# A two-layer graph kernel: layer 0's normalised rows transposed by DMA in place of TensorE, their head projection placed 20 blocks later, and the first attention selections on other buffers

## The chip, the cores and the metric

The kernel runs on one core of a Trainium2 chip. The metric is the device time of one execution in microseconds (us). Before the change it is 2277.46 us, the median of 3 runs (2276.98 to 2278.27).

The core's engines work side by side, each through its own queue in order: TensorE (PE in the profile; PEld is its weight load), VectorE (DVE), ScalarE (ACT), GpSimd (POOL) and SyncE (SP). SyncE and GpSimd issue the DMAs here, which run on 16 DMA engines.

## The reference

There are N = 3327 nodes with 1024 features each, and a sparse weighted adjacency `adj` (3327 x 3327). Two layers, each with a residual:

```python
# layer 0
h = maximum(layernorm(x), 0)
s = quant4(relu(quant4(h) @ quant(W0)))             # small integers
x1 = x + (adj / asf) @ s * (asf * delta)
# layer 1: attention with 8 heads of 64, over the edges of adj
h   = maximum(layernorm(x1), 0)
Wh  = einsum('nf,hfd->hnd', h, W)                   # 1024 -> 8 x 64
e   = leaky_relu(a1.Wh[i] + a2.Wh[j], 0.2), only where adj[i, j] > 0
out = elu(softmax(e) @ Wh)                          # then a dense part of four layers
x2  = x1 + mlp(out)
```

The change is about the step between the two layers: `layernorm(x1)`, its relu, and `Wh`.

## The kernel before, in words

Nodes are cut into T = 26 tiles of 128 rows. The work comes in four stages.

**Stage 1** (0 to 135 us): the quantised product of layer 0, `s_int[t]` for all 26 tiles, kept in SBUF. Its rows are transposed by DMA (line 300) as 128x1024 two-byte words.

**Stage 2** (135 to 974 us): for each tile t, `x1[t]` is the adjacency product: 26 blocks j, and in each block 4 matmuls of 128x512 (line 532): the adjacency block is split into a high and a low part (`hi`, `lo`) so that two fast passes give the accuracy, times two column halves. The blocks come in PARTS of 7, 6, 7 and 6. For each part the adjacency is loaded (`at`, three buffers, SyncE, line 183), `hi` is cast on ScalarE (line 187), `lo` and the 0/1 mask `mk` are made on VectorE (191, 192); `hi` and `lo` have two buffers each, so that `hi` of a part waits until TensorE is done with the part two before it. After a tile's blocks: `y` on ScalarE (547), then on VectorE a scale (548), the residual (549), the statistics and `half_normalised` (149 to 156), which gives (x1 - mean) / (2 sd).

`heads(t, y)` (line 463) then makes `Wh`: eight 128x128 TensorE transposes into PSUM (469), two evictions with relu and a factor of 2 into `ht` (470), eight 128x512 fp32 matmuls (473, two passes each) into `whm`, an eviction `wht` (475), the scores `src` and `dst` on VectorE (480, 481), a transpose of `src` (487), the exponentials (485, 497) and the features `ft`, `fw`, `dw` (498 to 511), written to DRAM by GpSimd (`src_d`, `feat_d`, `dsum_d`). The loop at 522 runs one tile behind: heads(t-1) is issued after tile t-1's normalisation and runs on TensorE among the first blocks of the next tile. A scheduler sets the order within each engine's queue when the program is built; `keep_in_program_order` fixes single instructions.

**Stage 3** (974 to 1976 us): attention. For each of 32 attends (a head and a group of 6 or 7 tiles), 26 steps j: VectorE makes `sel` (line 826, the mask where the score passes the leaky-relu's kink), TensorE multiplies it by the features `f_even` or `f_odd` into 7 accumulators (835). Between them come the edge sums (`all_edges`, 613): masks cast to `mf` on ScalarE (635) and multiplied by `dw` (636); `edge_steps(n)` (647) says how many of them are due by step n. The stage's loads are in SyncE's queue: masks of the first group, the source scores `srow` (601), features and sums of the tiles that are done, further masks, and the last tiles' features when they are written. They go to memory that `s_int` gives up, and to pools that follow stage 2's.

**Stage 4** (1976 us to the end): the dense part and the output.

Of the kernel before, what the change touches and what calls it, by code (L numbers as in the profile page):

```python
# [1 line left out]

# [6 lines left out]
F32 = mybir.dt.float32  # L9
BF16 = mybir.dt.bfloat16  # L10
F32R = mybir.dt.float32r
U8 = mybir.dt.uint8
I8 = mybir.dt.int8
AF = mybir.ActivationFunctionType
ALU = mybir.AluOpType
AX = mybir.AxisListType
PSUM = bass.MemoryType.PSUM
DRAM = bass.MemoryType.DRAM

P = 128  # L20
# [3 lines left out]
TH = T // 2  # L24
# [35 lines left out]
def two_layer_kernel(  # L60
# [83 lines left out]
    def plus_eps(var, n, tag, engine=nc.vector):  # L144
        v = small.tile([P, n], F32, tag=tag + "v", name=tag + "v")
        engine.tensor_scalar(v, var, EPS, None, ALU.add)
        return v

    def half_normalised(dst, src):

        stats = small.tile([P, FC, 6], F32, tag="stats", name="stats")
        statistics(stats, src)
        mv = small.tile([P, 2], F32, tag="mv", name="mv")
        nc.vector.bn_aggr(mv, stats.rearrange("p c s -> p (c s)"))
        r = half_inverse(plus_eps(mv[:, 1:2], 1, "ln"), 1, "ln")
        nc.vector.tensor_scalar(dst, src, mv[:, 0:1], r, ALU.subtract, ALU.mult)

    def scale_and_bias(rs, mean, n, factor, tag, engine=nc.vector):

        nb = small.tile([P, n], F32, tag=f"{tag}n", name=f"{tag}n")  # L160
        if engine is nc.vector:
            nc.vector.tensor_scalar(rs, rs, factor, None, ALU.mult)
            nc.vector.scalar_tensor_tensor(nb, mean, -1.0, rs, ALU.mult, ALU.mult)
        else:
            engine.tensor_scalar(rs, rs, factor, -1.0, ALU.mult, ALU.mult)
            engine.tensor_tensor(nb, mean, rs, ALU.mult)
            engine.tensor_scalar(rs, rs, -1.0, None, ALU.mult)
        return rs, nb

# [4 lines left out]
    with tc.tile_pool(name="at", bufs=2, reuse_waits="tile") as atp:  # L176
# [276 lines left out]
        with tc.tile_pool(name="wh", bufs=1, reuse_waits="tile") as whp, tc.tile_pool(  # L453
            name="s2", bufs=2, reuse_waits="tile"
        ) as s2, tc.tile_pool(name="mm", bufs=2, space=PSUM, reuse_waits="tile") as mm_ps, tc.tile_pool(
            name="s2_tp", bufs=2, space=PSUM, reuse_waits="tile"
        ) as tp_ps, tc.tile_pool(name="s2_wh", bufs=2, space=PSUM, reuse_waits="tile") as wh_ps:

            whead = whp.tile([P, KF, EMB], F32, name="whead")
            a1_t = whp.tile([P, EMB], F32, name="a1_t")  # L460
            a2_t = whp.tile([P, EMB], F32, name="a2_t")

            def heads(t, h):
                ht = s2.tile([P, KF, P], F32, name="ht", bufs=1)
                for g in range(KF // 4):
                    tp = tp_ps.tile([P, 4, P], F32, tag="tp2", name="tp2")
                    for q in range(4):
                        k = 4 * g + q
                        nc.tensor.transpose(tp[:, q, :], h[:, k * P : (k + 1) * P], ident)
                    nc.scalar.activation(ht[:, 4 * g : 4 * g + 4, :], tp, AF.Relu, scale=2.0)  # L470
                whm = wh_ps.tile([P, EMB], F32, name="whm")
                for k in range(KF):
                    nc.tensor.matmul(whm, ht[:, k, :], whead[:, k, :], start=(k == 0), stop=(k == KF - 1))  # L473
                wht = s2.tile([P, EMB], F32, name="wht", bufs=1)
                nc.scalar.copy(wht, whm)
                src = small.tile([P, NH], F32, name="src")
                dst = small.tile([P, NH], F32, name="dst")
                for a_t, e in ((a1_t, src), (a2_t, dst)):
# [4 lines left out]
                    )  # L483
                nc.vector.tensor_scalar(ndst[:, t], dst, -1.0, None, ALU.mult)
                nc.scalar.activation(ratio[:, t], src, AF.Exp, scale=1.0 - SLOPE)
                sp = tp_ps.tile([P, 4, P], F32, tag="tp2", name="sp")
                nc.tensor.transpose(sp[:NH, 0, :], src, ident)
                srct = s2.tile([NH, P], F32, name="srct")
                nc.scalar.copy(srct, sp[:NH, 0, :])  # L489
                for sub, d in zip(SUBS, src_d):  # L490
                    if t in sub:
                        nc.gpsimd.dma_start(d[:, (t - sub[0]) * P : (t - sub[0] + 1) * P], srct)
# [29 lines left out]
            for t in range(T):  # L522
                xt = s2.tile([P, F], F32, name="xt2")
                load_rows(xt, x, t)
                mm = mm_ps.tile([P, F], F32, tag="mm", name="mm2")
                for js in PARTS:
                    hi, lo = part
                    part = next(columns, None)
                    for q, j in enumerate(js):
                        for which in (hi, lo):  # L530
                            for c in range(FC):
                                nc.tensor.matmul(  # L532
                                    mm[:, c * 512 : (c + 1) * 512],
                                    which[:, q, :],
                                    s_int[j][:, c * 512 : (c + 1) * 512],
                                    start=(j == 0 and which is hi),
                                    stop=(j == T - 1 and which is lo),
                                )
                if t == 0:
                    for dst, ap in (  # L540
                        (whead, w_heads.rearrange("(k p) e -> p k e", p=P)),
                        (a1_t, a1.partition_broadcast(P)),
                        (a2_t, a2.partition_broadcast(P)),
                    ):
                        tc.keep_in_program_order(nc.sync.dma_start(dst, ap))
                y = s2.tile([P, F], F32, name="y")
                nc.scalar.activation(y, mm, AF.Copy, scale=r_asf)
                nc.vector.tensor_scalar(y, y, asf_t, sup_delta, ALU.mult, ALU.mult)
                nc.vector.tensor_tensor(xt, xt, y, ALU.add)
                nc.gpsimd.dma_start(x1_d[t * P : (t + 1) * P, :], xt)  # L550
                half_normalised(y, xt)
                if before is not None:
                    heads(*before)
                before = (t, y)
            heads(*before)
    supp.close()

# [9 lines left out]
    attends = [(c, g, e, si) for c, g in units for e in range(2) for si in range(2)]  # L567
    STEPS = 4 * T
    EDGE = 13 * T
    START = T - 2  # L570
    FRONT = 6
    LATE = 62
# [5 lines left out]
    dw = large(early, "dw", [P, T, HW], F32R)  # L578
    f_even = large(early, "f_even", [P, T, HW], F32R)
    masks[0] = large(early, "mask0", [P, 7, T, P], U8)  # L580
    with tc.tile_pool(name="sel", bufs=4, reuse_waits="tile") as selp, tc.tile_pool(
        name="srow", bufs=2, reuse_waits="tile"
    ) as srowp, tc.tile_pool(name="mf", bufs=2, reuse_waits="tile") as mfp, tc.tile_pool(
        name="md", bufs=2, reuse_waits="tile"
    ) as mdp, tc.tile_pool(name="f1", bufs=1, reuse_waits="tile") as f1p, tc.tile_pool(
        name="s3", bufs=1, reuse_waits="tile"
# [14 lines left out]
        def load_src(i):  # L601
            c, g, e, si = attends[i]
            nb = len(halves[c][si])
            srow = srowp.tile([P, 7, P], F32, name="srow")
            nc.sync.dma_start(
                srow[:, :nb].rearrange("p b i -> p (b i)"),
                src_d[2 * c + si][2 * g + e].partition_broadcast(P),
            )
            return srow

        def all_edges():

            for u, (c, g) in enumerate(units):
# [13 lines left out]
                for i in range(len(blocks)):  # L627
# [3 lines left out]
                    ps = m_ps.tile([P, 512], F32, tag="mps", name="mps")[:, :HW]  # L631
                    for j in range(T):
                        if j % TH == 0:
                            mf = mfp.tile([P, TH, P], F32R, tag="mf", name="mf")
                            nc.scalar.copy(mf, mask[:, j : j + TH, :])  # L635
                        nc.tensor.matmul(ps, mf[:, j % TH, :], dw[:, j, :], start=(j == 0), stop=(j == T - 1))  # L636
                        if j == T - 1:
# [9 lines left out]
        def edge_steps(n):  # L647

            if n < START:
                return min(n, START)  # L650
            if n < LATE:
                return START + (EDGE - START) * (n - START) // (LATE - START)
            u = min((n - LATE) // STEPS, len(units) - 2)
            m = n - LATE - STEPS * u
            span = STEPS + (LAST if u == len(units) - 2 else 0)

            first = min(T, max(0, (m - 6) * 2))
            rest = (EDGE - T) * max(0, m - 19) // (span - 19)
            return EDGE * (u + 1) + first + min(rest, EDGE - T)

# [59 lines left out]

        old, young = PARTS[:3], [range(20, 24), range(24, 25), range(25, 26)]
        load_mask(0, SUBS[0])
        srow = load_src(0)
        load_features(f_even, feat_d, 0, old)
        load_features(dw, dsum_d, 0, old)
        load_mask(1, SUBS[1])
        for js in young:
            load_features(f_even, feat_d, 0, [js])
            load_features(dw, dsum_d, 0, [js])
        load_features(f_odd, feat_d, 1, old + young)  # L730
        for i, (c, g, e, si) in enumerate(attends):
            if i == len(attends) - 1:

# [74 lines left out]
            sub, mask = halves[c][si], masks[si]  # L808
            nb = len(sub)
            f = f_odd if e else f_even  # L810
            srow_next = load_src(i + 1) if i + 1 < len(attends) else None
            accs = [acc_ps.tile([P, HW], F32, tag="acc", name="acc") for _ in sub]
            for j in range(T):
                n = i * T + j
# [7 lines left out]
                if n in (STEPS * NPAIR - T, STEPS * NPAIR):  # L822
                    si1 = (n - (STEPS * NPAIR - T)) // T
                    load_mask(si1, halves[1][si1])
                sel = selp.tile([P, 7, P], F32R, tag="sel", name="sel")
                nc.vector.scalar_tensor_tensor(  # L826
                    sel[:, :nb],
                    srow[:, :nb],
                    ndst[:, j, h : h + 1],
                    mask[:, :, j, :],  # L830
                    ALU.is_gt,
                    ALU.mult,
                )
                for b in range(nb):
                    nc.tensor.matmul(  # L835
                        accs[b], sel[:, b, :], f[:, j, :], start=(j == 0), stop=(j == T - 1)
# [125 lines left out]
```

## Time and profile before

| what | value |
|---|---|
| runs, median of 3 | 2277.46 us |
| the profiled execution's own time | 2277.77 us |
| its span | 2276.0 us |
| TensorE busy | 2219.2 us |
| VectorE, ScalarE, GpSimd busy | 1538.1, 978.7, 143.6 us |
| stage 2, one tile of 26 | 31.8 us |
| adjacency matmuls, line 532 | 2704 of 128x512 |
| heads' matmuls, line 473 | 416 passes of 128x512 |
| heads' TensorE transposes, line 469 | 208 of 128x128 |
| their evictions, line 470 | 52, mean 592 ns |
| DMA traffic | 311.47 MB, 137 GB/s over the span |
| granted TensorE clock, mean | 0.997 |

A group line of the profile gives the line of the code, the engine and operation, output <- inputs, shapes and count, then total busy time and the mean in ns of one, then the idle time of the engine ahead of them and what ended it. A line of the order of time gives start and length in us from the span's start, with runs of one kind merged. A TensorE matmul's length is longer than its spacing, since matmuls are pipelined: spacing is read from the starts. A line by windows gives, for each stretch, the busy us and the instructions of PE, PEld, DVE, ACT and POOL, then the granted TensorE clock (1.00 is full), the DMA share and GB/s.

### The profile page before, as it was taken

To read this page: it belongs to the slowest core of one execution; us is meant where nothing else is said; L and a number is where in the kernel's file an instruction comes from. 1 tells how busy PE (TensorE), PEld (TensorE's weight loads), DVE (VectorE), ACT (ScalarE), POOL (GpSimd) and SP (SyncE) were. 2 spreads that over 40 slices of the span, in tenths; PEclk is the share of its full clock that TensorE was granted. 3 is DMA by queue.
4 is the path that set the end of the run, shared out by engine and by line. 5 is a ranking of instruction groups with operands and counts; after the bars stand their busy time and mean duration, and the time that the engine had idled before them with its cause. 6 is when DMAs were issued, how large, how long until landed. Compare 5 with 4: busy or idle time off the path is not lost. (4 is left out here: it accounts for less than half of the span.)

```text
span 2276.0 us, 31632 instructions
## 1 busy us (share of the span) xinstructions
PE 2219.2 (98%) x12688; PEld 1772.3 (78%) x12696; DVE 1538.1 (68%) x1963; ACT 978.7 (43%) x1640; POOL 143.6 (6%) x241
## 2 busy tenths in 40 slices
PE   4999999999999999899999999999999999999998
PEld 1467777777777777589999999999999999744444
DVE  7745545555555455487999999999999999732211
ACT  5633333433343333346555555555555555311110
POOL 1300101011010111000000000000000000000000
PEclk9999999999999999999999999999999999999999
DMA  6854444454444544754233141654242422333311
GB/s 208 207 188 134 159 144 159 134 164 151 150 152 139 167 146 152 261 176 137 85 114 112 60 134 55 226 174 149 85 146 84 137 85 75 127 143 126 120 56 56
DMA packets 176579, 311.47 MB, mean 137 GB/s; under 512 B 36452, under 2 KB 117300, under 8 KB 176432
## 3 DMA queue, kind: packets, MB, share of 16 engines
q1 hardware_dynamic: 156648, 236.28, 32.0%
q0 software_dynamic: 19776, 73.17, 10.0%
q8 instruction: 99, 1.62, 0.3%
q14 instruction: 48, 0.39, 0.1%
q10 hardware_dynamic: 8, 0.00, 0.0%
HBM read 216.07 MB, written 86.79 MB: 133 GB/s over the span
## 5 line engine op out<-in xcount | busy, mean ns | idle before, releaser
L826 DVE SCALAR_TENSOR_TENSOR sel<-srow,ndst,mask 128x896 fp32r<-128x896 f32 (+1 forms) x832 | 864.1, 1080 | 51.4 <-PE acc L835 38.7
L636 PE MATMUL mps<-dw,mf 128*128 128x260 f32 x2704 | 454.9, 283 | 0.1
L532 PE MATMUL mm<-s_int,hi 128*128 128x512 f32 x1352 | 432.9, 399 | 0.0
L532 PE MATMUL mm<-s_int,lo 128*128 128x512 f32 x1352 | 421.8, 391 | 0.0
L835 PE MATMUL acc<-f_even,sel 128*128 128x260 f32 x2704 | 397.1, 284 | 0.1
L835 PE MATMUL acc<-f_odd,sel 128*128 128x260 f32 x2704 | 394.5, 286 | 0.0
L635 ACT CAST mf<-mask 128x1664 fp32r<-128x1664 uint8 x208 | 331.3, 1593 | 124.0 <-PE mps L636 101.2
L636 PEld LDWEIGHTS mps<-dw,mf 128*128 128x128 f32 x2704 | 378.2, 188 | 0.3 <-ACT part L640 0.3
L835 PEld LDWEIGHTS acc<-f_odd,sel 128*128 128x128 f32 x2704 | 352.8, 188 | 7.3 <-issue 3.4
L835 PEld LDWEIGHTS acc<-f_even,sel 128*128 128x128 f32 x2704 | 355.1, 188 | 2.9 <-ACT srct L489 0.3
L532 PEld LDWEIGHTS mm<-s_int,lo 128*128 128x128 f32 x1352 | 253.8, 188 | 57.6 <-issue 5.7
L532 PEld LDWEIGHTS mm<-s_int,hi 128*128 128x128 f32 x1352 | 252.1, 188 | 55.7 <-issue 5.7
L192 DVE TENSOR_SCALAR mk<-at 128x896 uint8<-128x896 f32 (+1 forms) x104 | 61.5, 593 | 257.2 <-DMA at<-in_adj_t 256.3
L187 ACT CAST hi<-at 128x896 fp32r<-128x896 f32 x104 | 92.6, 891 | 328.9 <-PE mm L532 294.8
L473 PE MATMUL whm<-whead,ht 128*128 128x512 f32 x416 | 187.1, 603 | 0.8 <-ACT ht L470 0.8
L906 PE MATMUL o<-weights,h 128*128 128x512 f32 x416 | 179.7, 592 | 0.0
L906 PEld LDWEIGHTS o<-weights,h 128*128 128x128 f32 x416 | 79.0, 190 | 99.1 <-issue 98.8
L473 PEld LDWEIGHTS whm<-whead,ht 128*128 128x128 f32 x416 | 77.5, 191 | 98.2 <-issue 88.1
L191 DVE TENSOR_TENSOR lo<-at,hi 128x896 fp32r<-128x896 f32 x104 | 106.6, 1025 | 58.9 <-ACT hi L187 49.4
L640 ACT COPY part<-mps 128x260 f32<-128x260 f32 x104 | 39.2, 377 | 221.5 <-PE mps L636 221.5
L916 DVE TENSOR_TENSOR yo<-o,nodes 128x1024 f32<-128x1024 f32 (+1 forms) x27 | 31.9, 1184 | 138.2 <-PE o L906 138.0
L423 PE MATMUL mm<-w_int,xqt 128*128 128x512 bf16 x408 | 95.4, 386 | 14.8 <-ACT sb L449 4.8
(154 smaller groups left out, 1519.7 us busy)
## 6 DMA issues: line engine op xcount, KB each, us to landing
feat_d<-fw POOLq DMA_DIRECT2D x26, 1040.0 KB, 5.4
f_even<-feat_d SPq DMA_DIRECT2D x7, 3380.0 KB, 13.3
f_odd<-feat_d SPq DMA_DIRECT2D x7, 3380.0 KB, 12.7
at<-in_adj_t SPq DMA_DIRECT2D x52, 448.0 KB, 4.4
at<-in_adj_t SPq DMA_DIRECT2D x52, 384.0 KB, 3.2
mask<-mask_d SPq DMA_DIRECT2D x39, 416.0 KB, 7.4
dw<-dsum_d SPq DMA_DIRECT2D x16, 910.0 KB, 8.8
dsum_d<-dw POOLq DMA_DIRECT2D x26, 520.0 KB, 6.5
```

The source lines that it names most:

```text
L187: ins = nc.scalar.copy(hi, at)
L191: nc.vector.tensor_tensor(lo, at, hi.bitcast(F32), ALU.subtract)
L192: ins = nc.vector.tensor_scalar(mk[:, r], at, 0.0, None, ALU.is_gt)
L423: nc.tensor.matmul(mm[:, r], xqts[t][:, k, :], w_int[:, k, r], start=(k == 0), stop=(k == KF - 1))
L473: nc.tensor.matmul(whm, ht[:, k, :], whead[:, k, :], start=(k == 0), stop=(k == KF - 1))
L532: nc.tensor.matmul(mm[:, c * 512 : (c + 1) * 512], which[:, q, :], s_int[j][:, c * 512 : (c + 1) * 512], start=(j == 0 and which is hi), s ...
L635: nc.scalar.copy(mf, mask[:, j : j + TH, :])
L636: nc.tensor.matmul(ps, mf[:, j % TH, :], dw[:, j, :], start=(j == 0), stop=(j == T - 1))
L640: nc.scalar.copy(part[:, i % 7], ps.rearrange("p (q c) -> p q c", q=2))
L826: nc.vector.scalar_tensor_tensor(sel[:, :nb], srow[:, :nb], ndst[:, j, h : h + 1], mask[:, :, j, :], ALU.is_gt, ALU.mult,)
L835: nc.tensor.matmul(accs[b], sel[:, b, :], f[:, j, :], start=(j == 0), stop=(j == T - 1))
L906: nc.tensor.matmul(ps[:, c * 512 : (c + 1) * 512], h3[:, k, q * P : (q + 1) * P], w4[:, k, c * 512 : (c + 1) * 512], start=(k == 0), stop= ...
```

## The change

It has these parts.

1. The normalised row is no longer scaled ahead of the projection: `normalised` makes max(x1 - mean, 0) in one VectorE instruction before the inverse deviation is known, and returns the factor r beside it; r is applied where `whm` is evicted.
2. For tiles 0 to 24 the row is transposed by DMA. DMA transposes two-byte words here, and the row is fp32, so ScalarE copies the row's 16-bit halves apart (`yh`, 128x2048 words), SyncE transposes them (`yht`), and ScalarE puts the halves together again (`ht`). Tile 25 keeps the TensorE transposes.
3. `heads(t-1)` is issued ahead of the last part of tile t, so after 20 of 26 blocks, and its first matmul and the eviction `wht` are held there.
4. PSUM: the transposes' pool goes; `sp` gets a bank of its own, and tile 25's transposes, `whm` and `sp` take turns in one bank. The buffer of `y` is single instead of double.
5. Stage 3: the pools of `mf`, `srow` and `sel` are laid out so that the first ones lie on the adjacency's buffers; `srow` is loaded ahead of the features; the edge sums begin at step 10, two a step; from step 4 on the first attend's selections are held behind tile 25's normalisation (`ln`).

In the queues of the built program, TensorE's order for a tile in the middle of stage 2 changes as follows (numbers are matmuls; the score transpose is `sp`).

```
before: transposes 8, adjacency 5, heads 8, adjacency 10, sp 1, adjacency 89
after:  adjacency 80, heads 8, adjacency 10, sp 1, adjacency 14
```

ScalarE's order for a tile after: `hi`, `fw`, `y`, `dw` twice, `hi`, `yh`, square root, `hi`, `ht`, `hi`, `wht`, exponentials. SyncE's: four `at`, the transpose, the x row.

```diff
-    def half_normalised(dst, src):
+    def normalised(dst, src):
         stats = small.tile([P, FC, 6], F32, tag="stats", name="stats")
         statistics(stats, src)
         mv = small.tile([P, 2], F32, tag="mv", name="mv")
         nc.vector.bn_aggr(mv, stats.rearrange("p c s -> p (c s)"))
+        ins = nc.vector.tensor_scalar(dst, src, mv[:, 0:1], 0.0, ALU.subtract, ALU.max)
         r = half_inverse(plus_eps(mv[:, 1:2], 1, "ln"), 1, "ln")
-        nc.vector.tensor_scalar(dst, src, mv[:, 0:1], r, ALU.subtract, ALU.mult)
+        nc.vector.tensor_scalar(r, r, 2.0, None, ALU.mult)
+        return ins, r
...
+    def halves_of_words(words):
+        return words.bitcast(U16).rearrange("p (n two) -> p two n", two=2)
...
+            def transposed_by_dma(y):
+                yh = s2.tile([P, 2, F], U16, name="yh", bufs=1)
+                nc.scalar.copy(yh, halves_of_words(y))
+                yht = s2.tile([P, 2 * KF, P], U16, name="yht", bufs=1)
+                nc.sync.dma_start_transpose(yht, yh.rearrange("p two f -> p (two f)"))
+                ht = s2.tile([P, KF, P], F32, name="ht", bufs=1)
+                nc.scalar.copy(
+                    halves_of_words(ht.rearrange("p k i -> p (k i)")),
+                    yht.rearrange("p (two k) i -> p two (k i)", two=2),
+                )
+                return ht
+            def transposed_by_tensor(y):
                 ht = s2.tile([P, KF, P], F32, name="ht", bufs=1)
                 for g in range(KF // 4):
-                    tp = tp_ps.tile([P, 4, P], F32, tag="tp2", name="tp2")
+                    tp = last_ps.tile([P, 4, P], F32, tag="last", name="tp2")
...
-                    nc.scalar.activation(ht[:, 4 * g : 4 * g + 4, :], tp, AF.Relu, scale=2.0)
-                whm = wh_ps.tile([P, EMB], F32, name="whm")
+                    nc.scalar.copy(ht[:, 4 * g : 4 * g + 4, :], tp)
+                return ht
+            def heads(t, ht, r):
+                if t == T - 1:
+                    whm, sp = (last_ps.tile([P, EMB], F32, tag="last", name=n) for n in ("whm", "sp"))
+                else:
+                    whm = wh_ps.tile([P, EMB], F32, name="whm")
+                    sp = sp_ps.tile([P, EMB], F32, name="sp")
                 for k in range(KF):
...
+                    if k == 0 and t < T - 1:
+                        tc.keep_in_program_order(ins)
                 wht = s2.tile([P, EMB], F32, name="wht", bufs=1)
-                nc.scalar.copy(wht, whm)
+                ins = nc.scalar.activation(wht, whm, AF.Copy, scale=r)
+                if t < T - 1:
+                    tc.keep_in_program_order(ins)
...
                 for js in PARTS:
                     hi, lo = part
                     part = next(columns, None)
+                    if js is PARTS[-1] and before is not None:
+                        heads(*before)
...
-                half_normalised(y, xt)
-                if before is not None:
-                    heads(*before)
-                before = (t, y)
+                ln, r = normalised(y, xt)
+                before = t, (transposed_by_tensor if t == T - 1 else transposed_by_dma)(y), r
             heads(*before)
...
+    FIRST = 10
...
-                return min(n, START)
+                return min(max(0, n - FIRST) * 2, START)
...
-        srow = load_src(0)
-        load_features(f_even, feat_d, 0, old)
+        srow, ins = load_src(0)
+        with tc.issue_after(ins.ins):
+            load_features(f_even, feat_d, 0, old)
...
+                with tc.issue_after(ln.ins) if i == 0 and j >= 4 else nullcontext():
+                    nc.vector.scalar_tensor_tensor(
```

## The prediction

> **What bounds the kernel now.** I read the page's first two parts, then the stage's groups by shape, then the order of time on TensorE across one tile boundary of layer 0 and across the passage to the attention stage, and last the DMA rows that stand nearest to what is new.
>
> ```profile
> PE 2219.2 (98%) x12688; PEld 1772.3 (78%) x12696; DVE 1538.1 (68%) x1963; ACT 978.7 (43%) x1640; POOL 143.6 (6%) x241
> ...
> PE   4999999999999999899999999999999999999998
> ```
>
> TensorE (PE) is busy 98% of the span, the others leave room. So time is won only where TensorE instructions go away or where it idles. It idles in slice 0 (the start, untouched) and in slice 16 (counted from 0), where the passage to attention begins at 945 us.
>
> ```profile
> 436.64 1.03 PE L469 MATMUL tp<-ident,y 128*128 128x128 f32 x8
> 437.43 0.71 PE L532 MATMUL mm<-s_int,hi 128*128 128x512 f32 x2
> 437.98 0.62 PE L532 MATMUL mm<-s_int,lo 128*128 128x512 f32 x2
> 438.44 0.39 PE L532 MATMUL mm<-s_int,hi 128*128 128x512 f32 x1
> 438.77 7.13 PE L473 MATMUL whm<-whead,ht 128*128 128x512 f32 x16
> 445.34 0.79 PE L532 MATMUL mm<-s_int,hi 128*128 128x512 f32 x1
> ...
> 468.44 1.03 PE L469 MATMUL tp<-ident,y 128*128 128x128 f32 x8
> ```
>
> One period of layer 0 (columns: start, length, line): 31.8 us from one row's transposes to the next. Starts matter, ends overlap. The eight transposes hold TensorE from 436.64 to 437.43, 0.79 us, and the pair behind them takes 0.55 where its fellows take 0.45. So a row's transposes cost 0.79 to 0.89 us, nothing beside them. (Near the end of the span 16 of the same kind take 1.75: 0.875 for eight. I use that.)
>
> ```profile
> 945.00:955.00 10.00, 8.73 (x28) 4.15 (x26) 3.69 (x6) 3.98 (x6) 0.55 (x1) 1.00 1.08 362
> 955.00:965.00 10.00, 1.49 (x8) 1.52 (x9) 7.09 (x11) 2.09 (x5) 0.54 (x1) 0.68 1.06 381
> 965.00:975.00 10.00, 9.28 (x19) 3.78 (x17) 3.48 (x7) 4.12 (x8) 1.69 (x2) 0.81 0.98 344
> ```
>
> The passage, ten us a row: busy us of PE, weight loads, VectorE (DVE), ScalarE (ACT), GpSimd; then granted clock, DMA share, GB/s. The last adjacency matmul ends at 945.57. Tile 24's heads fill until 954.6, then TensorE stands until 963.5: VectorE's first selection waits for the row of source scores (landed 957.9, the DMA queues are full), and tile 25's layer norm stands behind it.
>
> **The change, part by part.**
>
> *Transposes out of TensorE.* 25 of 26 rows: 25 x 0.875 = 21.9 us off TensorE. This is all on the path, if nothing new is late. The order of the built kernel shows it: each row now has 80 adjacency matmuls, 8 of the heads, 10 more, the score transpose, 14 more, in place of "8 transposes, 5, heads, 10, score transpose, 89".
>
> *Is the row's transposed copy there by block 20?* Let S be the tile's first matmul; a block is 4 matmuls of 0.2266 (pairs start every 0.453): 0.906. Heads are due at S + 18.1. The chain, by row durations in the order in which each engine's queue now has them: ScalarE: hi of the second part to S+0.6, fw 1.06, y 1.11, to S+2.8. VectorE: y 0.81, add 1.23, a mask 0.63, two statistics 1.29, aggregate 0.20, subtract 0.81, to S+8.05. ScalarE's hi of the third part stands ahead of the copy of halves and waits for block 7 (S+6.3, done 7.1), so the copy starts at 8.1.
>
> The two copies of 128x2048 16-bit words are not in the trace. The casts of 896 and 768 elements (945 and 837 ns) give 0.84 ns an element and 190 fixed, 1.91 us for 2048. One-byte input is no quicker (1664 in 1593, formula 1588) and gaps cost nothing (dw<-fw 520 in 631, formula 627), so below 1.9 there is no reason, and above it only if 16-bit halves went at half rate, 3.6. I take 1.91. The first copy ends at S+10.0.
>
> The nearest row for the DMA is layer 0's first product, which transposes 128x1024 two-byte words:
>
> ```profile
> L300 SPq DMA_TRANSPOSE xqt<-xq x25: 1231/1232/2122, 30.9 to 121.4; - x25
> ...
> DMA to landing us min/median/max: 3.1/3.1/6.8
> ```
>
> Issuing holds SyncE's queue 1.23 us, landing 3.1 from the start of issue. Twice the words: 2.46 to issue, and 2.46 + (3.1 - 1.23) = 4.35 to land; with the worst of the 25, 6.8 + 1.2 = 8. [...] I take 4.35[...]. Landing at S+14.4, second copy to S+16.4: 1.7 us before the heads are due. So no wait; the cover is thin, and each us beyond a landing of 6.05 costs 25 us.
>
> *Who is queued behind the new waits.* SyncE: the transpose waits for the copy (S+10.0) and holds the queue to 12.5; behind it are the next tile's x row and the adjacency parts, which in the trace arrive well over a tile part before use (three buffers): free. ScalarE: the second copy waits for the DMA; behind it is hi of the next part, which cannot start before S+17.9 anyway: free. Its added work is 2 x 1.91 less two evictions of 0.6, 2.6 us a tile on 11.9 of 31: free. VectorE: one more tensor_scalar (0.15 to 0.2): free. The lo of the third part comes at S+9.4 instead of earlier, due at 11.8. The score transpose keeps its 10 matmuls of cover, as now. GpSimd's queue keeps its order. DMA: the stage 100 to 122 us, mostly transposes, shows share 0.55 at 110 GB/s where 155 GB/s here is 0.47; I add about 0.1: free on average.
>
> *The passage.* Tile 24's heads now lie inside tile 25's blocks, so they no longer cover the passage, but the first selections can: they use the adjacency's buffers, the source scores are loaded ahead of the features, and four selections are allowed before tile 25's subtract. I compare lost time = elapsed less TensorE work, from the last adjacency matmul to the end of the first attend (182 matmuls).
> Before: 945.57 to 1006.2, 60.6 us. Work: two heads with transposes 15.7, 229 matmuls of 260 columns at 0.12, 27.4; lost 17.6.
> After, T = the last adjacency matmul: VectorE bounds it. It starts at T+1.6 (fw of tile 24, y on ScalarE), and has y 0.85, add 1.26, statistics 1.6, subtract 0.85, 26 selections at about 1.12 (1.15 alone, 1.05 chained) 29.1, scores 2.9, ft 1.3, fw 1.3, small ones 1.4: 40.6. It runs dry for 3.5 us while TensorE is in tile 25's heads (T+12.9 to 19.8; four selection buffers). The sum is T+45.7. Work: 0.9 + 6.9 + 0.1 + 212 x 0.12 = 33.3. Lost 12.4.
> The clock: [...] this trace, after 9 us of standstill, shows grants of 0.68 and 0.81 and those heads at 8.80 us instead of 6.87: 1.9 more. I take the trace: lost 14.4. Gain 17.6 - 14.4 = 3.2[...], and I lean up by 1 because some matmuls do run in those 13 us: 4.2.
> Masks and scores for the first selection: three or four of seven mask loads, and the scores, now stand behind tile 24's transpose on SyncE, to S+12.5; 2.1 MB at the 257 to 362 GB/s of these windows is 6 to 8 us, S+21; needed at T+3.4 = S+34. Free.
> *Edge sums.* They start 10 steps later, at two a step; the same number is done by step 24. Already in the work counts.
>
> **Sum.** 21.9 + 4.2 = 26.1. The profiled execution took 2277.77 (span 2276.0, 1.8 around it): 2251.7. The median of the runs, 2277.46, lies 0.3 lower: 2251.4.
>
> **Rivals.**
> 1. *The likeliest, as above*, 2245 to 2257: 0.63. For it: 13 or more of 25 transposes at the minimum of 3.1.
> 2. *Short waits in each tile* (landing 6.3 to 7, or ScalarE's order a little later than worked out): 0.3 to 0.9 us a row. At 0.6, 15 us: 2266. For it: feature writes, a 384 KB adjacency load and the transpose are under way together. 0.16.
> 3. *Slower*: the transpose lands late each tile, and TensorE waits ahead of the heads at block 20. The point from which it decides: 26.1 / 25 = 1.04 us of wait, a landing of 7.1 us after issue. At the row's worst, scaled to 8, the wait is 1.95 and 25 x 1.95 = 49: 2300. For it: the 6.8 in the row; copies at half rate would do the same. Against: median equals minimum while 512 KB loads were under way. 0.09.
> 4. *Passage no better*: first selection waits for its masks on VectorE, ahead of tile 25's statistics, as now. 4 to 8 us lost: 2257. 0.12. Against: 13 us of slack.
> That the order isn't as said is excluded by the built order.
>
> **Numbers.** Within 0.2% (4.6 us, about what a measurement can tell from no change) is 2273 to 2282. Faster: case 1, 4, and nearly all of 2: 0.88. Same: 0.04. Slower: 0.08. The range: below 2244 only if the passage loses half of what I reckon; above, case 2 up to 2268; left out are case 3 and tails.
>
> **What would show it.** No TensorE transposes in layer 0 but tile 25's; a period of 30.9 us; no wait of the heads on the second copy. Copies 1.9 us each. Transposes landing 4 to 6 us after issue. Between the last adjacency matmul and the first attend's end 46 to 48 us, TensorE starting selections within 5. Wrong if the heads wait, if the period stays near 31.8, or if VectorE's first selection waits for a DMA.

## The result, and the profile after

The changed kernel takes 2258.87 us, the median of 4 runs (2256.93 to 2262.46), beside 2277.86 (2276.98 to 2278.30) before: a ratio of 0.9918, 95% interval 0.9905 to 0.9932. The gain is 19.0 us; forecast were 26.1 (2251.4), with a range up to 2268. The profiled execution took 2258.69, its span is 2256.9.

The page's busy times:

```profile
PE 2199.3 (97%) x12496; PEld 1753.9 (78%) x12496; DVE 1532.4 (68%) x1989; ACT 1062.0 (47%) x1642; POOL 145.0 (6%) x241
```

TensorE has 19.9 us less work. ScalarE has 83 us more, and it hurts nowhere by its sum. One period of layer 0, in order of time on TensorE (start, length, line), without a wait:

```profile
488.92 7.03 PE L502 MATMUL whm<-whead,ht 128*128 128x512 f32 x16
495.38 1.03 PE L568 MATMUL mm<-s_int,hi 128*128 128x512 f32 x2
...
519.64 7.03 PE L502 MATMUL whm<-whead,ht 128*128 128x512 f32 x16
```

From heads to heads 30.72 us, where before it was 31.81. Not every row goes like that; the heads of another row, which wait 1.10 us, and the sum over TensorE's waits (us in total, times, longest):

```profile
769.35 7.13 PE L502 MATMUL whm<-whead,ht 128*128 128x512 f32 x16 [1.10 <-ACT ht L479]
```

```profile
PE whm L502 <- ACT ht L479: 6.8, 10, 2.1
PE acc L876 <- issue: 5.0, 1, 5.0
```

In 10 of 25 rows the heads wait for the joined row. The 24 periods from the first heads to the 25th sum to 747.4 us, 10.1 more than 24 x 30.72. That is more than the 6.8 of the waits: behind a wait the heads start from an idle TensorE and take up to 6.57 us to the next adjacency matmul in place of 6.46, and a wait's idle time counts only from the modelled end of the matmul before it. The chain that ends there, by line 477 (issue of the transpose in ns, then landing, min/median/max) and by ScalarE's two copies (busy us and mean ns ahead of the idle time):

```profile
L477 SPq DMA_TRANSPOSE yht<-yh x25: 3246/3630/5720, 167.9 to 914.3; - x25
...
DMA to landing us min/median/max: 5.2/5.8/8.1
```

```profile
L479 ACT COPY ht<-yht 128x2048 uint16<-128x2048 uint16 x25 | 62.6, 2506 | 85.5 <-DMA yht<-yh 85.5
L475 ACT COPY yh<-y 128x2048 uint16<-128x2048 uint16 x25 | 47.5, 1900 | 20.7 <-DVE y L156 20.7
```

The first copy has its 1.91 us. The second takes 2.51 in place of 1.91, and the transpose lands after 5.8 in place of 4.35. (The trace has the landings of 17 of the 25; the joining copies, of all 25, begin 5.8 us after the issue in the median.) The row is later than reckoned by 0.6 + 1.45 = 2.05, somewhat more than the slack of 1.7: in the median the joined row is complete 18.1 us after the tile's first matmul, just when the heads are due.

The passage, ten us a row (busy PE, weight loads, VectorE, ScalarE, GpSimd, then granted clock, DMA share, GB/s):

```profile
935.00:945.00 10.00, 4.67 (x20) 3.59 (x19) 8.72 (x13) 6.19 (x8) 2.68 (x4) 0.77 1.09 359
945.00:955.00 10.00, 9.87 (x42) 7.74 (x43) 7.27 (x12) 1.38 (x3) 0.00 (x0) 0.71 1.03 411
```

The last adjacency matmul ends at 937.37, the first selection's matmuls begin at 942.53, 5.2 us later (5.0 by the trace's count of idle time), and the hole of 9 us is gone. From the last adjacency matmul to the end of the first attend (182 selection matmuls) it is 47.0 us, before 59.3 when counted alike. Tile 24's heads and transposes (7.6) and 14 matmuls of edge sums at 0.12 (1.7) have left that stretch, so the passage itself gained 12.3 - 9.3 = 3.0.

### The profile page after: what moved, and what is told of

Read it like the earlier page. It is cut to its first block, busy times and chain, and to the rows that moved or that the text cites. A ratio compares the mean times of both kernels' runs of the same rounds, so it can differ in the third digit from the quotient of the medians.

```text
span 2256.9 us, 31286 instructions
## 1 busy us (share of the span) xinstructions
PE 2199.3 (97%) x12496; PEld 1753.9 (78%) x12496; DVE 1532.4 (68%) x1989; ACT 1062.0 (47%) x1642; POOL 145.0 (6%) x241
## 5 line engine op out<-in xcount | busy, mean ns | idle before, releaser
L568 PE MATMUL mm<-s_int,hi 128*128 128x512 f32 x1352 | 427.1, 397 | 0.0
L957 DVE TENSOR_TENSOR yo<-o,nodes 128x1024 f32<-128x1024 f32 (+1 forms) x27 | 31.8, 1182 | 137.6 <-PE o L947 137.4
## 6 DMA issues: line engine op xcount, KB each, us to landing
f_even<-feat_d SPq DMA_DIRECT2D x7, 3380.0 KB, 12.3
```

Source lines behind the costliest of these rows:

```text
L568: nc.tensor.matmul(mm[:, c * 512 : (c + 1) * 512], which[:, q, :], s_int[j][:, c * 512 : (c + 1) * 512], start=(j == 0 and which is hi), s ...
```

## The experiments

Twelve kernels beside the changed one. Theory A: what the forecast lacks is the row's late arrival, by the transposing DMA (what shares the DMA engines with it, or its size) and by the joining copy. Rival: TensorE's saving was over-reckoned, or the passage gave less. (Letters in the expectations stand for the theories as they stood when each was written.)

**Heads three blocks later.** 2.7 us more cover, if nothing else moves.

```diff
-                    if js is PARTS[-1] and before is not None:
-                        heads(*before)
                     for q, j in enumerate(js):
+                        if js is PARTS[-1] and q == (3 if t < T - 1 else 0) and before is not None:
+                            heads(*before)
```

> The heads of tiles 0 to 23 stand 3 blocks later (after 23 of 26); tile 24's stay at block 20, everything else as in the changed kernel. Theory A (the row's transposed copy comes late for block 20, because the DMA transpose takes 5.8 us to land instead of 4.35 and the joining copy 2.5 instead of 1.91): 3 blocks are 2.7 us of cover, more than the longest wait of 2.1, so the waits of TensorE on the joining copy (8.8 us in all by the gaps before the heads) go, all but tile 24's 1.4: 2258.9 - 7.4 = 2251.5, every period 30.8, and the spread of the runs shrinks. Rival B (the copy is late because the stage's engines or DMA queues are loaded, and what is waiting moves along with the heads): waits of like size at the new place, 2257 to 2259.

2296.5 us (2291.94 to 2297.8), ratio 1.0076 (1.0062 to 1.0089): slower than before the change, and both expectations missed. The transpose's landing and TensorE's wait:

```profile
DMA to landing us min/median/max: 7.9/8.1/8.4
```

```profile
PE whm L502 <- ACT ht L479: 32.1, 24, 4.6
```

Later heads make their own features later. VectorE's `ft` and `fw` of the row before now stand ahead of the next row's statistics (the copy `yh` begins 9.8 us after the tile's first matmul in the median, in place of 7.9), and GpSimd issues `x1`, the features and their sums (2 MB) at 486.4 to 488.9, right ahead of the transpose at 492.7. The trace has only 6 of the 25 landings, but all 25 joining copies, which begin 8.0 us after the issue in the median and 10.6 at the worst. The copy moves by 1.9 and the landing by 2.2: 4.1 us lost for 2.7 of cover.

**The transpose in two.** Is it its size?

```diff
-                nc.sync.dma_start_transpose(yht, yh.rearrange("p two f -> p (two f)"))
+                for w in range(2):
+                    nc.sync.dma_start_transpose(yht[:, w * KF : (w + 1) * KF], yh[:, w])
```

> The one DMA transpose of 128x2048 words is issued as two of 128x1024 in a row, after the same copy; nothing else changes. Theory A1 (one transpose of 2048 words is dearer than two of 1024, as 3.2 to 3.6 us of issue against 1.23 in stage 1 suggest): 1.23 to 1.4 us of issue each, both landed 4.4 us after the first issue, 1.4 us earlier than now: nearly all waits of the heads go, 2251 to 2253. Theory A2 (the same transpose is slower in stage 2 than in stage 1 because of the other traffic): issue of the two together still 3.2 to 3.6 us, landing 5.8, 2257 to 2260.

2258.53 (2256.61 to 2260.05), ratio 0.9915 (0.9902 to 0.9929): no change. Each half issues in 1.23 to 3.95 us (median 1.66), the heads wait 7.5 us. Cutting it changes nothing. What is left to test is the traffic beside it.

**A second copy without gaps.** One more copy of `yht` behind the joining one, into plain words (`nc.scalar.copy` from `yht` to `yh`).

> Adds one ScalarE copy of 128x2048 16-bit words behind the joining copy in each of 25 tiles, from the transposed words to a free buffer, both sides without gaps; nothing uses it. It measures the disputed cost by itself. Theory G (gaps of a word in the output make the joining copy slower): the plain copy takes 1.9 us beside the joining copy's 2.5. Rival: both take 2.5 (the source, written by DMA, or the word type costs it). Its 1.9 us come behind the joining copy and ahead of a cast not due for 10 us, so the time stays within 2 us of 2258.9.

```profile
L479 ACT COPY ht<-yht 128x2048 uint16<-128x2048 uint16 x25 | 62.7, 2507 | 85.4 <-DMA yht<-yh 85.4
...
L483 ACT COPY yh<-yht 128x2048 uint16<-128x2048 uint16 x25 | 47.3, 1891 | 0.0
```

The same source and size: 1.89 us plain and 2.51 where each 16-bit word is written into every other place. `yh<-y`, which reads with gaps and writes plainly, has 1.90. So it is the output's gaps that cost 0.62 us. (2258.2 us, one run.)

**Heads three blocks earlier** (at 17 of 26).

> The changed kernel with the heads 3 blocks earlier, after 17 of 26 blocks. The joined row is there at about 18.2 us after the tile's first matmul, the heads would be due at 15.4: a wait of 2.8 us a row if the landing stays at 5.8 us, 70 us in all less the 8.8 of now: 2320. The features and their writes move ahead by the same 2.7 us, away from the transpose; if the landing falls with that to 4.5, the wait is 1.5: 2287. This is the slower case of the prediction, brought about by less cover instead of a later landing.

2378.11 us (one run), 58 more than the worse expectation. The landing fell as said:

```profile
DMA to landing us min/median/max: 4.2/4.4/5.2
```

```profile
L502 PE MATMUL whm<-whead,ht 128*128 128x512 f32 x416 | 224.2, 700 | 85.2 <-ACT ht L479 85.2
```

Yet the heads wait 85.2 us, 3.4 a row, and then their matmuls take 700 ns in place of 596: 39.8 us more. 78.4 more of waiting and 39.8 of slow heads are 118.2 of the 119.4 by which the span grew. Two things were not in either expectation. The mask of an adjacency part now stands on VectorE between statistics and aggregate and waits 2.5 us for its DMA (at 555.19), so that the copy starts later (10.0 us after the tile's first matmul in the median, in place of 7.9). And behind most of these waits TensorE is slow (19 of 25 rows; the last section comes back to this): the stretch 634 to 647 has a clock of 0.74 granted.

**TensorE transposes for all rows**, the rest as changed (two PSUM banks in turn, no copies of halves).

> The changed kernel with TensorE transposes for all tiles (two PSUM banks in turn, 33 matmuls into the next tile) in place of the DMA's and of the two word copies; heads still after block 20, attention's start as changed. It undoes one part. Theory A: 25 x 1.02 us (31.82 less 30.8 of undisturbed period) come back and 8.8 us of waits go: 2258.9 + 25.5 - 8.8 = 2275.6. Rival C (the DMA transposes also slow TensorE or its queue elsewhere, so that they save less than the period says): 2268 to 2271. By the 0.875 us per row of the prediction it would be 2272.

2287.12 (2285.39 to 2287.31), ratio 1.0039 (1.0027 to 1.0052), 11.5 over the expectation. It is no clean measure: with the transposes at their new place TensorE waits for VectorE's subtraction (9.0 us over 23 rows), and the first selections too. The period is 32.3.

**Halves in turn.** Copy, transpose and join each half-word plane by itself, so that they overlap.

```diff
+                htw = halves_of_words(ht.rearrange("p k i -> p (k i)"))
+                for w in range(2):
+                    nc.scalar.copy(yh[:, w], halves_of_words(y)[:, w])
+                    nc.sync.dma_start_transpose(yht[:, w * KF : (w + 1) * KF], yh[:, w])
+                for w in range(2):
+                    nc.scalar.copy(htw[:, w], yht[:, w * KF : (w + 1) * KF].rearrange("p k i -> p (k i)"))
```

> The changed kernel with the row's two half-word planes copied, transposed and joined one after the other, so that the first transpose starts while the second plane is still being copied, and the first join runs while the second transpose is under way. If the lateness is the length of the chain (copy 1.9, landing 5.8, join 2.5), about 2 us of it now overlap and the heads' waits vanish: 2250. If the second transpose lands behind the same traffic at 6 us or more after its issue, waits of 0.2 us a row remain: 2254 to 2256.

2252.26 (2251.89 to 2254.01), ratio 0.9890 (0.9875 to 0.9904). Heads wait 2.7 us, in 3 rows. A shorter chain alone takes most of the waits away.

**The tile's writes behind the transpose.** The features, their sums and `x1`, issued by SyncE behind the transpose.

```diff
-                nc.gpsimd.dma_start(x1_d[t * P : (t + 1) * P, :], xt)
...
+                    with tc.issue_after(ins.ins):
+                        if t:
+                            write()
+                        nc.sync.dma_start(x1_d[t * P : (t + 1) * P, :], xt)
```

> The changed kernel with the feature writes and the x1 write of a tile (2 MB) issued by SyncE right behind the tile's transpose instead of by GpSimd just ahead of it; nothing else moves. Theory A (the transpose lands late because those writes share the DMA engines with it): the median landing falls from 5.8 us to 4.4 to 5, the issue below 3 us, the heads no longer wait (8.8 us now), 2250. Rival B (the landing is the transpose's own, or due to the adjacency loads): landing stays at 5.5 to 6 us, heads wait 7 to 9 us, 2257 to 2260.

2269.19 (2267.45 to 2273.79), ratio 0.9968 (0.9955 to 0.9980): slower than the changed kernel, as neither expected. Landing 5.3 in the median, and the heads' waits are down to 1.9 us (2 rows), but a new wait has come. TensorE's wait, then SyncE's queue in order of time:

```profile
PE sp L521 <- DVE src L516: 15.5, 23, 1.9
```

```profile
583.42 1.31 SPq L598 DMA_DIRECT2D x_d<-xt  x1
584.84 1.17 SPq L190 DMA_DIRECT2D at<-in_adj_t  x1
590.67 0.33 SPq L126 DMA_DIRECT2D xt<-in_x  x1
```

The next x row's load waits until 590.67, when the `x1` write issued at 583.42 (landing 7.2 us) has left its buffer. The adjacency part behind it, asked for at 591.11, comes late, its mask on VectorE (594.95) stands ahead of the score products, and the score transpose on TensorE waits. To test this reading, only the features were moved and `x1` left with GpSimd:

> The changed kernel with only the feature writes behind the transpose on SyncE; the x1 write stays with GpSimd where it was. In the run that moved both, TensorE waited 15.5 us for the scores. My reading: there the next x row's load waits in SyncE's queue for its buffer, which the late x1 write still holds, and adjacency parts behind it come late, so that VectorE's mask of them, ahead of the score products, does too. If that is so the waits for the scores vanish here (under 2 us) and the heads' waits stay small (transposes landing 5.2 to 5.6): 2250 to 2253. If instead the issue of 1.5 MB by SyncE ahead of the adjacency parts makes them late, the waits for the scores stay at 10 us or more: 2262 to 2269.

2251.77 (2251.61 to 2252.14), ratio 0.9886 (0.9871 to 0.9901).

```profile
DMA to landing us min/median/max: 4.5/4.6/6.0
```

The waits for the scores are 0.7 us, those of the heads 0.8. The transpose of 128x2048 lands in 4.6 us: the forecast's 4.35 nearly, and earlier than the 5.2 to 5.6 expected here. But not all of the 1.2 us gained can be put down to the writes, since the order of SyncE's queue changed with them. Around one transpose, the changed kernel first, then this run:

```profile
510.44 0.33 SPq L190 DMA_DIRECT2D at<-in_adj_t  x1
511.31 3.60 SPq L477 DMA_TRANSPOSE yht<-yh  x1
```

```profile
506.79 2.77 SPq L477 DMA_TRANSPOSE yht<-yh  x1
...
510.96 1.24 SPq L190 DMA_DIRECT2D at<-in_adj_t  x1
```

In the changed kernel an adjacency part is issued 0.9 us ahead of the transpose, here 4.2 us behind it. The run before had all three writes behind the transpose and the adjacency part still 0.9 us ahead of it: 5.3. So about 0.5 us of the landing go with the writes, and the other 0.7 with the adjacency part, or with the `x1` write, which here lands 1.7 us before the transpose is issued. That these loads and writes delay it, and not GpSimd's queue as such, the heads at block 17 show too: there the features stay with GpSimd but are issued 10 us and more ahead of the transpose, the adjacency part stands behind it, and it lands in 4.4.

**Both** (halves in turn, and all three writes behind the second transpose):

> Both: planes in turn, and the tile's writes behind the second transpose. With either cause removed the heads have 2 us or more of slack; no wait of the heads on the joined row: 2249 to 2251, the same as the better of the two alone, since a wait can only be taken away once. Under 2248 would mean that writes or joins cost something else as well.

2250.03 (2249.13 to 2252.40), ratio 0.9880 (0.9865 to 0.9895), the interval below the changed kernel's. Its periods are 30.72 but for a few early and late rows (2.9 us in 24 periods). The `x1` write is with SyncE here too, lands as late (7.8 us after its issue in the median), and the x row's load waits for it as long. But the built order has the adjacency part ahead of that load, at 20.0 us after the tile's first matmul in place of 22.2, and the waits for the scores are 1.7 us in all. So it is what stands behind the load in the queue that did the harm, not the late write alone.

**Eight transposes put back** into that last version, directly ahead of the heads, their result unused:

> The version without waits (planes in turn, writes behind the transpose, 2250.0) with eight TensorE transposes of 128x128 fp32 put back directly ahead of the heads of tiles 0 to 24; they transpose a block of the weights and nothing reads the result, so no copy and no wait comes with them. It measures what eight transposes a row cost TensorE by themselves. By the prediction's term, 0.875 us a row: 25 x 0.875 = 21.9, 2271.9. By the difference of the undisturbed periods (31.81 before, 30.72 now), 1.09 a row: 27.2, 2277.3. Transposes between two kinds of fp32 matmuls: if the 0.2 us difference is the change of kind at the heads, and not the transposes, it comes out at the lower value.

2270.53 (2268.73 to 2272.12): 20.5 more. Every period is 31.60, so eight cost 0.88 us there (25 x 0.88 is 21.9; the version beside it had 2.9 us of longer periods, this one has none):

```profile
586.30 1.04 PE L504 MATMUL tp<-ident,whead 128*128 128x128 f32 x8
587.18 7.03 PE L507 MATMUL whm<-whead,ht 128*128 128x512 f32 x16
```

The lower value holds, 0.875. The other 0.21 us a row by which the period fell is a wait of the kernel before, and its trace shows where. TensorE's own waits do not list it; those of the weight loads (PEld) do, once in every row:

```profile
PEld whm L473 <- ACT ht L470: 10.1, 26, 1.1
```

The heads' first weights are the transposed row in `ht`, and their load starts when the first eviction ends, 0.05 us earlier; that eviction stands behind `y` on ScalarE, and five adjacency matmuls don't cover it. In the lines shown, the matmul ahead of the heads takes 0.33 us in place of 0.23 (438.44 to 438.77), and the heads take 6.57 to the next adjacency matmul (438.77 to 445.34) in place of the 6.46 of the changed kernel (488.92 to 495.38): 0.21 together. Here, with the transposes back and no eviction, both are gone.

**The attention stage's start of before**, on the version without waits and on the changed kernel as it is (old pools, scores among the features, no holding back, edge sums from step 0):

> The version without waits (2250.0) with the attention stage's start as it was before the change: the pools of selections, scores and mask copies in their old order, the scores loaded among the features, no holding back of selections, edge sums from step 0. It undoes the passage part alone. If that part is worth what the prediction's sum gave by the trace's row, 3 us: 2253; with its lean 4.2: 2254.2. If the gain in the passage comes from the heads having moved into the last tile, and the edits of the attention stage do nothing: 2250. If without them the first selections stand behind full DMA queues as before, with nothing now to fill TensorE (9 us of standstill less 5.0 now): 2254 to 2258.

> The changed kernel as it is, with the attention stage's start of before alone (old order of the pools, scores among the features, no holding back, edge sums from step 0). On the version without waits this made no difference (2249.7 beside 2250.0). Same here: 2258 to 2260. If the early load of the scores matters where GpSimd writes the features and x1 ahead of the transpose, as in the changed kernel, the first selections come later by some us: 2261 to 2264.

Without waits: 2249.70 (2247.91 to 2251.11), ratio 0.9878 (0.9863 to 0.9892), no difference. On the changed kernel: 2265.86 (2263.61 to 2268.34), ratio 0.9949 (0.9932 to 0.9966), 7.0 slower, more than I allowed. There SyncE is held by tile 24's transpose until 921 and by the features until 937:

```profile
914.85 6.13 SPq L477 DMA_TRANSPOSE yht<-yh  x1
921.02 2.51 SPq L633 DMA_DIRECT2D mask<-mask_d  x5
...
937.47 2.50 SPq L639 DMA_DIRECT2D srow<-src_d  x1
```

```profile
949.85 2.21 DVE L860 SCALAR_TENSOR_TENSOR sel<-srow,ndst,mask 128x896 fp32r<-128x896 f32 x2 [5.11 <-DMA mask<-mask_d]
```

The scores are asked for at 937.5 (in the changed kernel at 922.8), and the first selection runs at 949.85 (941.3). The trace names a mask as what came last, but the first group's masks were all issued by 923.5, and the last one issued landed at 929.4; the scores, issued behind the features, are what the selection still lacked. In the version without waits the transposes hold SyncE 1.25 us each and end by 911, so that even in the old order the scores are asked for at 924.9, and the edits have nothing to save.

## Why the prediction was right in sign and 7 us too good

*Transposes out of TensorE: right, and too small.* 0.875 for eight was right (0.88 when put back). What failed is "nothing beside them": the kernel before also waited 0.21 us a row for their eviction, so the period fell by 1.09: 27.2 in place of 21.9. Half of this was in the lines I showed: a single matmul ahead of the heads that takes 0.33 in place of 0.23. I took it for nothing.

*The row there by block 20: the step that failed.* "Landing at S+14.4, second copy to S+16.4: 1.7 us before the heads are due. So no wait." Two terms were too small. The landing took 5.8, not 4.35, because of what is under way beside it: 2 MB of writes (features of the row before and `x1`), issued 4.7 to 6.7 us ahead of it, and an adjacency part issued 0.9 ahead. With all the writes behind it, it takes 5.3; with the features and the adjacency part behind it, and `x1` landed before, 4.6. I had the features and that part as evidence for a rival and put the average DMA share in the sum, 0.47 and about 0.1 for the change. The changed kernel has 0.58 over 200 to 900, but 0.83 in the 5.8 us from the issue of the first transpose and 0.98 to 1.19 for the other 24. The row from stage 1 spoke for it more than I saw: I read 3.1 as the landing of 13 or more of 25 transposes, but the trace has the landings of only 11, of which 7 lie at 3.05 to 3.2 and 4 at 4.2 to 6.8. The joining copy took 2.51, not 1.91: "gaps cost nothing" came from a copy of 4-byte words in runs of 65 (`dw<-fw`), and I used it for 16-bit output with a gap behind every word. Together they use up the slack, and the periods grew by 10.1 us; the version without these waits is 8.8 us faster. Rival 2 thus took place in part, beside the mechanism forecast. Its mean of 0.6 us a row was 0.4.

*Who is queued behind the new waits: free, as said, in the passage only with the attention edits.* "Masks and scores for the first selection ... Free" holds (five masks stand behind the transpose, not three or four) because the scores are loaded ahead of the features. Without that edit the transpose's hold on SyncE costs 7.0 us there.

*The passage: 3.0, where I reckoned 3.2 and leaned to 4.2.* The lean was an estimate that no trace showed, and the nearness is partly luck: 1006.2, which I took for the end of the first attend before, lies in the second (the 182nd selection matmul ends at 1005.0), so that the lost time before was about 16.5 and my sum should have given about 2. Elapsed 47.0, within the 46 to 48 forecast, first selections after 5.2. The clock did fall, to 0.52 of full in 940 to 950, but on the first selections' few matmuls; tile 25's heads ran at full speed (7.13 us), not at 8.80. Lost time came from VectorE, as reckoned.

The sum: 27.2 - 10.1 + 3.0 = 20.1 beside 19.0 measured. Of the 1.1 left over, 0.3 lie ahead of stage 2's first matmul, and 0.3 in the last full period before, which was 31.5 and not 31.8; the rest isn't placed. That the forecast came as near as 7 us owes something to luck: the transposes gave 5.3 more than forecast, and the waits took 10.1.

*Slower, rival 3:* the experiment with heads at block 17 shows it, and worse than its price: a wait of 3.4 us a row (0.3 in the changed kernel) cost 4.7, since behind 19 of 25 of them the heads took 8.0 to 9.5 us in place of 6.57.

## What to carry to other kernels

When a transfer goes into a chain with 1 or 2 us of slack, look at which transfers are issued in the few microseconds ahead of it, and size its landing by those, not by the stage's mean share: here it was 5.8, 5.3 or 4.6 us by what stood ahead. When an edit moves one transfer, compare the built order of the whole queue before putting the gain down to that transfer: here the adjacency part had gone from 0.9 us ahead of the transpose to 4.2 behind it. Moving its consumer later bought no cover here, where the consumer's own output is what collides with it (4.1 us lost for 2.7 of cover): shorten the chain (halves in turn, 2252.26) or issue the bulk writes behind it (the features and their sums, 2251.77). Before moving a write to another queue, ask whose buffer it holds, which load in that queue will wait for it, and what stands behind that load: with `x1` moved too, TensorE waited 15.5 us for the scores. And when a matmul group starts late by a tenth of a microsecond, look at the waits of its weight loads as well: before the change they came to 10.1 us for the heads.

## What the hardware showed that I had not expected

- ScalarE copies 2048 16-bit words in 1.89 us into plain places and in 2.51 into every other one; the copy with gaps on the input side alone took 1.90.
- In four runs the issue of a transpose of 128x2048 words held SyncE's queue longer where the transpose landed later: in the median 1.9 us with heads after block 17 (landing 4.4), 2.8 with the features behind (4.6), 3.6 in the changed kernel (5.8) and 5.9 with heads after block 23 (8.1). The least was 1.7, the most 8.4, in the first and the last of these.
- With heads after block 17, TensorE waited 2.0 to 4.2 us ahead of them. In 19 of 25 rows they then took 8.0 to 9.5 us to the next adjacency matmul, in the other 6 the 6.57 of full speed. The length of the wait doesn't settle which. Two rows of that run, each with a wait of 3.10 us, in two stretches each (TensorE's busy us come first, the clock third from the end):

```profile
280.48:283.89 3.41, 0.52 (x3) 0.09 (x1) 0.46 (x2) 2.31 (x1) 0.00 (x0) 1.00 0.94 278
283.89:287.30 3.41, 3.20 (x4) 1.51 (x5) 0.77 (x2) 0.15 (x1) 0.00 (x0) 0.50 0.03 8
```

```profile
314.61:318.02 3.41, 2.04 (x10) 1.35 (x8) 1.43 (x5) 1.32 (x2) 0.00 (x0) 1.00 1.10 238
318.02:321.44 3.42, 1.68 (x4) 0.87 (x5) 1.19 (x2) 1.69 (x1) 0.00 (x0) 1.00 0.35 136
```

Around the first wait TensorE is busy 0.52 us of the first stretch at a clock of 1.00, and the second stretch has 0.50. Around the other it is busy 2.04 and 1.68 us, and the clock is 1.00 in both. What decides between the two was not shown. In the changed kernel the heads' waits were up to 2.1 us, and no heads of tiles 0 to 24 were slow: 6.46 to 6.57 us to the next adjacency matmul, at a granted clock of 1.00 over 167 to 937.
